# The end of a four-image attention and expert kernel in another order

## Chip, core and metric

The kernel runs on one core of one Trainium2 chip. Times are microseconds (us) of device time for the whole program. Engines are called as in the profile: PE (TensorE matmuls; PEld are its weight loads), DVE (VectorE), ACT (ScalarE), POOL (GpSimd), and SP, whose queue only issues transfers. A q behind a name (SPq) is the engine's queue. L497 is line 497 of the kernel before.

## What is computed

```python
# layer 0, x: (4, 32, 128, 128); 128 channels of 4096 positions per image
q = space_to_depth(x)                       # (b, 4096, 128) as the products use it
energy = q @ q.T / (|q_i| |q_j|)            # 4096 x 4096 per image, symmetric
x = gamma * (softmax(energy) @ q) + q       # turned back to (4, 32, 128, 128)
# layer 1, on 32 x 128 = 4096 rows (tokens) of 128 per image
t = t + linear_attention(ln(t))             # heads 8, out = Q (K^T V)
p, i = top_k(softmax(ln(t) @ router_w + router_b), 2); p = p / sum(p)
t = t + sum_k p_k * (ln(t) @ expert_w[i_k] + expert_b[i_k])      # 8 experts
```

All data are 32-bit floats. The attention of layer 1 is linear, so a Gram matrix of the normalised rows (128x128) stands for all of K^T V.

## The kernel before

**Four images in turn.** `attend(b)` does layer 0 of image b. It goes through the lower triangle of 512x512 blocks: a matmul into `pe` (L609), an exponential on ACT with row sums (L612), and two uses of the result: as weights for the values `po` (L497), and, turned by DVE (L421) and sent through DRAM on SP's queue (`blocks`, L530 and L545), for the mirrored block `pg` (L433). A mirrored block is used when a clock of planned PE work (`clock[0]`) has gone 57 units (`LAG`) past the issue of its transfer; a unit is about 0.25 us.

**Layer 1 beside it.** `layer1(b)` returns generators. While image b + 1 is in `attend`, layer 1 of image b is stepped every `PACE` = 10 units. For the last image (b = 3, `alone` in the code) there is nothing to hide it under: `close_rows` starts when its inputs are there, and `last_parts` comes after everything else. PE, DVE, ACT and SP run in the order in which the program issues (`manual_schedule`); on POOL, what is marked `pinned` keeps its order.

**Image 2 and the gathers.** For images 0 to 2, tokens are sorted by expert: POOL writes rows to DRAM with 32 scatters for each half of the rows (`DMA_INDIRECT`, L1053), SP loads them as tiles (L1083), PE multiplies each tile with its expert's weights (L1117), SP stores the results (L1103), and POOL gathers two results for each token (L1165). For image 2 (`b == B - 2`), `gather_apart` gathers into `yb`, eight for a group of four rows of tokens (`k`); DVE adds them to `acc` (L1200) and SP stores (`put`, L1159). Its second half (h = 1) has groups 4 to 7, so 32 gathers, and comes last. Every scatter and gather waits for the newest exponential (`exps`).

**The end of image 3.** The 32 rows `k` (128 tokens each) are closed in four batches of eight, kc = 0 to 3, by `close_rows`:

- denominators `den`, `rd`, `wide` (L747 to L752, DVE); transposes of them into `pbd` (L774, PE); `divide` into `df` (L761, DVE); the addition to T (L783); statistics (L786);
- `close_stats`: six small DVE operations (L682 to L688), then on POOL a power (L164) and one or two more (L690, L692), which give `rsa`, `nba` (or `rsf`, `nbf`, `nbo` for the second norm);
- `normalise` (ACT, L696) or, for four of the eight rows of kc = 2 and 3, a DVE operation (L796); the Gram product (L728) and its addition (L724); transposes to `xnT` (L701, copied by ACT, L714). `keep_running` (L186) fills PE with transposes that nobody reads.

`last_parts` then does, in program order: `matrix` (L839 to L843); attention of row groups u = 0 and 1 with their statistics (L854, L1309, L1317); of u = 2 and 3, copied by ACT to `copies` (L1311); logits of rows 0 to 15 (`router_rows`, 8 operations) and gates (`route(0)`, about 15); and the loop over k = 0 to 31. A step of the loop scales the eight products of row k with its gates: the last n = `by_scalar(k)` on ACT (L1247) and the rest on DVE (L1233). PE is two rows ahead with `py` (L1290, four matmuls of 0.43 us per row). Every second step POOL sums what ACT made (`sum_rows`, L1255 to L1259); every fourth, SP stores (L1265). Rows 16 to 31 get statistics, logits and gates from `second_half`, stepped once per k. The order of two pieces is plain from these lines:

```python
                if k < 8:
                    normalise(range(8 + k, 9 + k), rsf, nbo)
                    if k % 4 == 3:
                        transpose_tokens(2 + k // 4)()
                if k >= 1:
                    next(rest, None)
```

Of the kernel before, what the change touches and what calls it, by code (L numbers as in the profile page):

```python
# [22 lines left out]
def kernel(  # L23
# [43 lines left out]
    nc = tc.nc  # L67
# [586 lines left out]
    def layer1(b, st):  # L654
# [76 lines left out]
        def close_rows(kc):  # L731
# [18 lines left out]
            for s in range(2):  # L750
                one = rd[:, ts(s, NJ)][:, :, None]
                nc.vector.tensor_scalar(wide[:, :, s], one.to_broadcast([P, NJ, 64]), gam, None, ALU.mult)  # L752
            df = work.tile([P, 8, HW2, 2], F32, tag="df", name=f"df_{b}_{kc}", bufs=1)
# [31 lines left out]
            for j in range(8):  # L785
                stats[j]()  # L786
                if j == 3:
                    yield
                    yield
            close_stats("a", 8 * kc, 8, bs)  # L790
            yield from idle(1 if late_rows else 3)
            k = 8 * kc
            normalise(range(k, k + 4), rsa, nba)
            if late_rows:
                for j in range(k + 4, k + 8):
                    nc.vector.tensor_scalar(  # L796
                        xn[:, j, :D], T[:, j, :], rsa[:, j, :], nba[:, j, :], ALU.mult, ALU.add
                    )
            yield
            if last_rows:  # L800
                keep_running(36)
                done = gram_rows([k + j // 2 + 4 * (j % 2) for j in range(8)])
                yield
                done()
                return
# [70 lines left out]
        def route(h, temps=None):  # L876

            sh = [P, KT // 2, E]
            rows = slice(h * KT // 2, (h + 1) * KT // 2)
            ms, dn = (stat.tile([P, KT // 2, 1], F32, tag=nm, name=f"{nm}_{b}_{h}") for nm in ("ms", "dn"))  # L880
            pr = stat.tile(sh, F32, tag="prob", name=f"prob_{b}_{h}", bufs=1)
# [40 lines left out]
        def transpose_tokens(g, alloc=psum_t):  # L922

            pt, done = hold(
                f"ptf_{b}_{g}",
                lambda p: nc.scalar.activation(xn[:, ts(g, 4), :D], p.rearrange("p (j t) -> p j t", t=P), AF.Copy),
                alloc,
            )
            for j in range(4):
                nc.tensor.transpose(pt[:, ts(j, P)], xn[:, 4 * g + j, :D], ident)  # L930
            return done

        def attention_rows(u):
# [32 lines left out]
            if u % 2:  # L966
                for _ in route(u // 2):
# [6 lines left out]
        def sorted_experts(h):  # L974
# [72 lines left out]
            for n in range(2 * HR):  # L1047
# [14 lines left out]
                wait_for(inst.ins, exps, "not more of these at a time than steps have")  # L1062
                scatters.append(inst.ins)
# [97 lines left out]
            groups = list(range(r0 // 4, (r0 + HR) // 4))  # L1161

            def gather(to, g, i, j, op):
                k = 4 * g + j
                inst = nc.gpsimd.indirect_dma_start(to, None, ys, offset(place[:, i, k : k + 1]), compute_op=op)  # L1165
                wait_for(pinned(inst).ins, exps, "not more of these at a time than steps have")

# [17 lines left out]

            def gather_apart():
# [15 lines left out]

                for g in groups:
                    yb[g] = work.tile([P, 2, 4, D], F32, tag="wide", name=f"yb_{b}_{g}")
                    after_steps.append((now[0] + 1, partial(fetch, g)))
                    for n in range(8):
                        gather(yb[g][:, n // 4, n % 4, :], g, n // 4, n % 4, ALU.bypass)
                        if n == 7:
                            after_steps.append((now[0] + 4, partial(combine, g)))
                        if n % 2:  # L1210
                            yield
                            yield
                            due()
                turns[h].append("gathered")
# [23 lines left out]
        def scaled_rows(k, py, n=4):  # L1238

            if k % 2 == 0:  # L1240
                nm = f"tmp_{b}_{k // 2}"
                if n <= 4:
                    tmps[k // 2] = work.tile([P, 2, n, D], F32, tag="wide", name=nm)
                else:
                    tmps[k // 2] = fpool.tile([P, 2, n, D], F32, tag="F", name=nm)
# [15 lines left out]
        def store(g):  # L1261
            for r1 in range(2):
                for s in range(2):
                    p0 = s * 64 + r1 * 32
                    nc.sync.dma_start(dst[s, r1, :, ts(g, 4), :], accs[g][p0 : p0 + 32])  # L1265
# [9 lines left out]
        def last_parts():  # L1275
# [9 lines left out]
            def by_scalar(k):  # L1285

                return 6 if k < 8 else 5 if k < 14 else 4
# [4 lines left out]

            for _ in matrix():
                pass

            la = fpool.tile([P, KT, 2 * E], F32, tag="F", name=f"la_{b}")
            copies = {}

            def attended(u):
                if u >= 2:  # L1300
                    copies[u] = fpool.tile([P, 8, D], F32, tag="F", name=f"pac_{b}_{u}")
                for j0 in range(0, 8, 3):
                    pa = bank(f"pat_{b}_{u}_{j0}")
                    attend_rows(u, j0, pa)
                    nj = min(3, 8 - j0)
                    pr = pa[:, : nj * (D + 2 * E)].rearrange("p (j d) -> p j d", d=D + 2 * E)
                    if u < 2:
                        tg = T[:, 8 * u + j0 : 8 * u + j0 + nj, :]
                        nc.vector.tensor_tensor(tg, tg, pr[:, :, :D], ALU.add)  # L1309
                    else:  # L1310
                        nc.scalar.activation(copies[u][:, j0 : j0 + nj], pr[:, :, :D], AF.Copy)  # L1311
                    nc.scalar.activation(la[:, 8 * u + j0 : 8 * u + j0 + nj, :], pr[:, :, D:], AF.Copy)

            def stats_of(u):
                bs, stats = batch_stats("f", 8 * u, 8)
                for f in stats:
                    f()  # L1317
                close_stats("f", 8 * u, 8, bs)

            attended(0)  # L1320
            stats_of(0)
            transpose_rows(6)()
            transpose_rows(7)()
            attended(1)
            stats_of(1)
# [172 lines left out]
```

## Time and profile before

| what | value |
|---|---|
| median of 3 runs | 1663.79 us (1658.05 to 1667.66) |
| the profiled execution's own time | 1659.2 us |
| its span, first to last instruction | 1657.4 us |
| PE busy | 1623.1 us (98%), 5288 matmuls |
| DVE, ACT, POOL busy | 917.4, 910.4, 596.2 us |
| scatters and gathers on POOL | 192 of about 0.97 us; 128 of 1.59; 64 of 0.97 |

The page gives shares of the whole span. PE's share is high because layer 0 of the next image covers layer 1 of the one before; the last image has no such cover. What the end costs is therefore read from stretches of the span, each with its own limit: busy time of an engine close to the stretch's length marks the limit, and the waits say what the others wait for. PEclk is the share of PE's clock that was granted. PE's busy time includes filler transposes and is partly modelled.

### The profile page before, as it was taken

Reading aid. Unit: us, or ns where it says so; the run is one execution under the profiler, and the core shown is the slowest. Engines: PE = TensorE matmul, PEld = TensorE weight load, DVE = VectorE, ACT = ScalarE, POOL = GpSimd, SP = SyncE. Lnnn points to the kernel's source line nnn. Section 1 sums busy time; section 2 is a strip of 40 time slices with the busy share of each in tenths; the row PEclk is TensorE's granted clock in tenths of the full one; section 3 lists DMA queues with packets and bytes.
Section 4 is the critical chain, followed back from the end, with each engine's and each line's share of the span. In section 5 each row is a group of like instructions: output and inputs, shape, how many; then the busy total and the mean of one; then the engine's idle time right before and its main releaser. Section 6 shows DMA issues by size and latency. Waiting matters only on the chain.

```text
span 1657.4 us, 21471 instructions
## 1 busy us (share of the span) xinstructions
PE 1623.1 (98%) x5288; PEld 856.9 (52%) x5288; DVE 917.4 (55%) x2359; ACT 910.4 (55%) x2863; POOL 596.2 (36%) x565
## 2 busy tenths in 40 slices
PE   8999999999999999999999999999999999999987
PEld 5444544455554455555564455555565445554643
DVE  4543353567486443559378453448559533344686
ACT  3555445566575555556575455556657455555376
POOL 1000000001014531456555543346546642436166
PEclk9999999999999999999999999999999999999999
DMA  4555656665349776986778868797668877885001
GB/s 147 199 181 174 198 186 213 230 212 170 131 171 277 246 220 213 271 249 176 207 200 254 265 208 255 214 287 200 167 196 239 277 222 246 240 254 168 15 14 39
DMA packets 241899, 332.81 MB, mean 201 GB/s; under 512 B 31984, under 2 KB 168304, under 8 KB 227440
## 3 DMA queue, kind: packets, MB, share of 16 engines
q1 hardware_dynamic: 207312, 291.92, 55.5%
q0 software_dynamic: 26624, 25.58, 7.5%
q10 hardware_dynamic: 7840, 13.93, 2.8%
q8 instruction: 45, 0.74, 0.2%
q14 instruction: 78, 0.64, 0.1%
HBM read 160.78 MB, written 175.80 MB: 203 GB/s over the span
## 4 chain that ended last, share of the span: by engine, by line
PE 84%; DMA 4%; DVE 4%; SPq 3%; ACT 2%; issue 2%; another core or an unknown queue 1%; POOL 0%; ACTq 0%; DVEq 0%; POOLq 0%
PE po L497 24%; PE pe L609 23%; PE pg L433 20%; PE pys L1117 3%; DMA blocks<-F 3%; PE py L1290 3%; PE pg L453 2%; SPq L545 2%; PE pat L854 2%; PE pys L1124 2%; PE pgram L728 1%; PE ptx L701 1%; DVE df L761 1%; PE pgv L839 0%
## 5 line engine op out<-in xcount | busy, mean ns | idle before, releaser
L612 ACT ACTIVATE pr<-pe 128x512 f32<-128x512 f32 (+1 forms) x576 | 322.4, 560 | 544.0 <-PE pe L609 448.2
L497 PE MATMUL po<-pr,qT 128*128 128x512 f32 (+3 forms) x1152 | 549.6, 559 | 4.2 <-ACT o L502 3.0
L609 PE MATMUL pe<-qn,qn 128*128 128x512 f32 x896 | 459.6, 595 | 2.6 <-ACT pr L612 1.6
L433 PE MATMUL pg<-F,qT 128*128 128x512 f32 x880 | 449.7, 592 | 1.1 <-DMA F<-blocks 1.1
L421 DVE STREAM_TRANSPOSE F<-pr 128x512 f32<-128x512 f32 x440 | 305.9, 702 | 144.8 <-ACT pr L612 127.0
L497 PEld LDWEIGHTS po<-pr,qT 128*128 128x128 f32 x1152 | 215.3, 190 | 251.7 <-issue 221.2
L1165 POOL DMA_INDIRECT acc<-ys,place x128 | 203.2, 1588 | 215.8 <-ACT pr L612 140.3
L438 ACT ACTIVATE junk<-F 128x512 bf16<-128x512 f32 x440 | 273.0, 620 | 1.2 <-DMA F<-blocks 1.2
L433 PEld LDWEIGHTS pg<-F,qT 128*128 128x128 f32 x880 | 166.7, 190 | 195.4 <-issue 181.0
L1053 POOL DMA_INDIRECT xs<-xn,place x192 | 186.0, 969 | 189.7 <-ACT pr L612 116.6
L609 PEld LDWEIGHTS pe<-qn,qn 128*128 128x128 f32 x896 | 155.0, 191 | 115.0 <-issue 104.6
L442 DVE TENSOR_TENSOR o<-o,pg 128x512 f32<-128x512 f32 x110 | 75.3, 684 | 207.9 <-PE pg L433 173.4
L1099 DVE TENSOR_TENSOR results<-pys,xn 128x256 f32<-128x256 f32 x120 | 49.9, 416 | 187.1 <-ACT xn L1093 122.0
L164 POOL TENSOR_TENSOR rn<-ss,neg_half 128x8 f32<-128x8 f32 (+1 forms) x17 | 27.2, 1602 | 320.9 <-DVE ss L296 320.8
L612 ACT ACTIVATION_READ_ACCUMULATOR pr<-pe 128x1 f32 x576 | 112.0, 194 | 0.0
L1093 ACT ACTIVATE xn<-pys 128x256 f32<-128x256 f32 x120 | 45.2, 377 | 112.5 <-PE pys L1124 94.5
L1117 PEld LDWEIGHTS pys<-ew_sb,xn 128*128 128x128 f32 x468 | 70.4, 191 | 53.0 <-issue 49.5
L1165 POOL DMA_INDIRECT yb<-ys,place x64 | 61.8, 965 | 84.5 <-DMA F<-blocks 31.1
L609 PE MATMUL pe<-qn 128*128 128x512 f32 (+3 forms) x256 | 90.2, 435 | 0.7 <-ACT qn L342 0.7
L438 ACT ACTIVATION_READ_ACCUMULATOR junk<-F 128x1 f32 x440 | 84.6, 192 | 0.0
L1117 PE MATMUL pys<-ew_sb,xn 128*128 x468 | 71.7, 275 | 0.4 <-ACT xn L1093 0.4
L164 POOL TENSOR_TENSOR rsa<-dm_a,neg_half 128x8 f32<-128x8 f32 x16 | 28.9, 1807 | 103.1 <-DVE sv_a L688 102.9
(216 smaller groups left out, 1521.1 us busy)
## 6 DMA issues: line engine op xcount, KB each, us to landing
blocks<-F SPq DMA_DIRECT2D x110, 1024.0 KB
F<-blocks SPq DMA_DIRECT2D x220, 192.0 KB
F<-blocks SPq DMA_DIRECT2D x220, 128.0 KB
xn<-xs SPq DMA_DIRECT2D x114, 132.0 KB
ys<-results SPq DMA_DIRECT2D x114, 128.0 KB
F<-blocks SPq DMA_DIRECT2D x220, 64.0 KB
below<-F SPq DMA_DIRECT2D x31, 384.0 KB
T<-in_x_dram SPq DMA_DIRECT2D x64, 128.0 KB
```

Source lines behind the costliest of these rows:

```text
L164: pinned(nc.gpsimd.tensor_tensor(dst, src, neg_half.to_broadcast(list(src.shape)), ALU.pow))
L421: f()
L433: nc.tensor.matmul(pg.rearrange("p (a f) -> p a f", a=4), st["qT"][i][:, ib, :], G[:, :, ib], start=(ib == 0), stop=(ib == NJ - 1),)
L438: nc.scalar.activation(junk, G[:, :, ib], AF.Copy, accum_out=st["sums"][:, NJ * i + ib, jc : jc + 1])
L442: nc.vector.tensor_tensor(st["o"][jc], st["o"][jc], pg, ALU.add)
L497: nc.tensor.matmul(row["po"][:, lo:hi], qT[blk // NJ][:, blk % NJ, :], w, start=start, stop=(row["left"] == 0))
L609: nc.tensor.matmul(pe[:, c0:], qn[jc][:, ts(j, P)], qn[i][:, c0:], start=True, stop=True)
L612: nc.scalar.activation(pr[:, c0:], pe[:, c0:], AF.Exp, accum_out=sums[:, t, i : i + 1]).ins
L1053: inst = nc.gpsimd.indirect_dma_start(xs[h], offset(place[:, i, k : k + 1]), xn[:, k, :], None)
L1099: nc.vector.tensor_tensor(result[:, :n], p[:, 2 * P : 2 * P + n * D].rearrange("p (j c) -> p j c", c=D), bufs[g % 6][:, :n, D : D + 1].to_ ...
L1117: nc.tensor.matmul(p[:, 2 * P + j * D : 2 * P + j * D + D], bufs[6 + g % 2][:, j, :D], weights[:, bass.ds(begins[2 * (g % 2) + j], D)], st ...
L1165: inst = nc.gpsimd.indirect_dma_start(to, None, ys, offset(place[:, i, k : k + 1]), compute_op=op)
```

## The change

For image 3: batch kc = 2 holds its statistics back until kc = 3 has its denominators; ACT normalises all eight rows of kc = 2 and three of kc = 3 (DVE the other five); the filler falls from 36 to 10 transposes; Gram products take eight rows at a time. For image 2: group 7's eight gathers and half of group 6's leave `gather_apart` and are issued in `close_rows` of image 3, four in kc = 2 and eight in kc = 3; their additions and stores go into the last loop; every fourth scatter or gather waits for the four before it. In `last_parts`, gates come for rows 0 to 7 first, for 8 to 15 in steps 4 to 7 of the loop, and for 16 to 31 in steps 10 to 15. GpSimd normalises rows 2 to 15 and adds the `copies`; ACT takes six experts for k below 16 and four from there; the last stores go over two queues.

```diff
 def close_rows(kc):
...
+            if last_rows:
+                st["all_divided"] = True
...
+            while late_rows and "all_divided" not in st:
+                yield from idle(1)
             close_stats("a", 8 * kc, 8, bs)
-            yield from idle(1 if late_rows else 3)
+            if late_rows:
+                for _ in range(8 if last_rows else 4):
+                    states[b - 1]["gathers"].pop(0)()
+            yield from idle(1 if alone else 3)
             k = 8 * kc
-            normalise(range(k, k + 4), rsa, nba)
-            if late_rows:
-                for j in range(k + 4, k + 8):
+            normalise(range(k, k + (3 if last_rows else 8 if late_rows else 4)), rsa, nba)
+            if last_rows:
+                for j in range(k + 3, k + 8):
                     nc.vector.tensor_scalar(
...
             if last_rows:
-                keep_running(36)
-                done = gram_rows([k + j // 2 + 4 * (j % 2) for j in range(8)])
+                keep_running(10)
+                done = gram_rows([k + j for j in (3, 0, 4, 1, 5, 2, 6, 7)])
                 yield
                 done()
+                return
+            if late_rows:
+                done = gram_rows(range(k, k + 8))
+                turned = [transpose_rows(g) for g in (4, 5)]
+                yield
+                for done in (done, *turned):
+                    done()
                 return
...
-        def route(h, temps=None):
+        def route(r0, nr, temps=None):
...
-        def transpose_tokens(g, alloc=psum_t):
+        def transpose_tokens(k0, n):
...
+                if b == B - 2 and n % 4 == 0:      # scatters
+                    wait_for(inst.ins, scatters[-4:], "a pause after each fourth")
...
+                if b == B - 2 and j == 0:          # gathers
+                    wait_for(inst.ins, gathered[-4:], "a pause after each fourth")
+                gathered.append(inst.ins)
...
+            def fetch_late(g):
+                accs[g] = buffer("acc", g)         # in the pool of pr
+                nc.sync.dma_start(accs[g], t2[:, ts(g, 4)])
...
+            def leave_for_the_end(g):
+                made = []
+                gathers.extend(partial(gather_late, g, n, made) for n in range(8))
+                gathers[-8:] = [lambda f=gathers[-8]: (fetch_late(g), f())] + gathers[-7:]
+                sums_left.extend(partial(add_late, g, lambda i=i: made[i]) for i in range(2))
+                sums_left.append(partial(put, g))
...
+                if h == 1:
+                    leave_for_the_end(groups.pop())
...
+                        if apart and n == 4:       # the last group that is left
+                            break
...
+                if h == 1:
+                    leave_half_for_the_end(groups[-1], yb[groups[-1]])
...
-                return 6 if k < 8 else 5 if k < 14 else 4
+                return 6 if k < 16 else 4
...
+            transpose_rows(6)()
             for _ in matrix():
                 pass
+            transpose_rows(7)()
...
+            bs0, stats0 = batch_stats("f", 0, 8)
+            bs1, stats1 = batch_stats("f", 8, 8)
+            for j0 in (0, 3, 6):
+                attended(0, j0)
+            some_stats(stats0, 0)
+            some_stats(stats0, 4)
+            close_stats("f", 0, 8, bs0)
+            logits = router_rows(nc.vector, 0, 8, la[:, :8])
+            next(logits)
+            for u in (1, 2):
+                for j0 in (0, 3, 6):
+                    attended(u, j0)
+            normalise(range(0, 2), rsf, nbo)
+            pinned_rows = range(2, 8)
+            normalise_apart(pinned_rows)           # nc.gpsimd.tensor_scalar, a row each
+            for _ in logits:
+                pass
+            attended(3, 0)
+            attended(3, 3)
+            transpose_tokens(0, 2)()
+            attended(3, 6)
+            gates = route(0, 8)
+            next(gates)
+            for u in (2, 3):
+                tg = T[:, ts(u, 8), :]
+                pinned(nc.gpsimd.tensor_tensor(tg, tg, copies[u], ALU.add))
+            products = [product(0, h, bank(f"py_{b}_0_{h}")) for h in range(2)]
+            transpose_tokens(2, 2)()
+            some_stats(stats1, 0)
+            for _ in gates:
+                pass
+            transpose_tokens(4, 4)()
+            products += [product(1, h, bank(f"py_{b}_1_{h}")) for h in range(2)]
...
+            rest = rest_of_rows()                  # stats1, close, stats, router, route(8, 8), ...
+            left = list(states[b - 1]["gathers"]) + list(states[b - 1]["sums_left"])
             for k in range(KT + 4):
+                if 2 <= k < 6:
+                    normalise_apart(range(4 + 2 * k, 6 + 2 * k))
...
+                    if k in (4, 6):
+                        transpose_tokens(2 * k, 4)()
...
-                    store(k // 4 - 1)
+                    store(k // 4 - 1, (nc.sync, nc.scalar) if k > KT else (nc.sync, nc.sync))
...
+                if 11 <= k < 25:
+                    normalise(range(2 * k - 6, 2 * k - 4) if k < 13 else range(k + 7, k + 8), rsf, nbo)
+                if k in (12, 16, 20, 24):
+                    transpose_tokens(k + 4, 4)()
+                if 17 <= k and left:
+                    left.pop(0)()
+                next(rest, None)
```

## Prediction

> **What bounds the kernel now.** I read the page's first part, then a table of stretches over the last 155 us, then the waits, the chain of waits and the timeline inside each stretch. The page has TensorE (PE) busy for 1623.1 of 1657.4 us, and the timeline shows fewer than 12 us of PE gaps (over 0.25 us each) before 1500 us. So nothing done before 1500 us can give much, and the question is what the end is worth:
>
> ```profile
> core 0: us, PE busy (x) PEld busy (x) DVE busy (x) ACT busy (x) POOL busy (x), PEclk, DMA share, GB/s
> 1502.00:1547.50 45.50, 42.08 (x131) 21.65 (x131) 29.79 (x80) 24.90 (x78) 24.79 (x25) 0.96 0.38 106
> 1547.50:1565.90 18.40, 15.29 (x105) 13.65 (x103) 11.67 (x38) 7.47 (x17) 2.78 (x4) 0.91 0.06 15
> 1565.90:1570.40 4.50, 3.96 (x23) 3.10 (x23) 1.59 (x4) 0.51 (x1) 0.00 (x0) 1.00 0.01 4
> 1570.40:1588.50 18.10, 15.91 (x96) 12.12 (x96) 15.77 (x64) 9.45 (x31) 4.76 (x6) 1.00 0.00 0
> 1588.50:1602.80 14.30, 12.56 (x29) 4.33 (x30) 13.19 (x39) 13.16 (x48) 9.60 (x9) 1.00 0.04 10
> 1602.80:1621.60 18.80, 17.37 (x45) 6.40 (x44) 14.34 (x48) 17.02 (x57) 17.75 (x21) 1.00 0.13 30
> 1621.60:1650.80 29.20, 27.88 (x70) 12.15 (x68) 22.42 (x64) 22.63 (x79) 23.51 (x27) 1.00 0.18 41
> 1650.80:1657.40 6.60, 0.00 (x0) 0.00 (x0) 1.54 (x3) 0.00 (x0) 0.00 (x0) 0.67 0.18 41
> ```
>
> I put the borders at events: the last value matmul (1547.5), the last Gram sum (1565.9), the first attention matmul (1570.4), and rows 0, 8 and 16 of the expert loop. In 1570–1588 DVE leads (15.8 of 18.1). In the loop's first half ACT leads (13.2 of 14.3, 17.0 of 18.8) with POOL beside it; in its second half PE leads. A busy PE is partly filler: the chain has
>
> ```profile
> 1558.79 5.00 PE spare L186 x36
> 1563.79 1.80 PE pgram L728 x16
> ```
>
> where the rows for the Gram product were ready at 1562.4 (end of the four ACT rows of L696).
>
> In the first stretch, the waits of 1515–1530 are
>
> ```profile
> DVE df L761 <- remote: 5.4, 1, 5.4
> ACT pr L612 <- PE pe L609: 4.7, 1, 4.7
> ...
> ACT pr L612 <- remote: 3.3, 1, 3.3
> ```
>
> DVE and ACT were freed within 0.05 us of each other at 1528.05, though the matmuls they waited for stand at 1523.3–1523.7: the news of the matmuls came late. Each ACT wait of over 2.6 us between 1285 and 1530 has seven or more gathers or scatters in the 12 us before it, mostly 1.25–1.3 us apart. The gathers of 1416–1468, mostly alternating 1.25 and 2.0 us, have no such wait. PE lost 1.0 us (at 1502) and 2.4 us (at 1527) by it, and then
>
> ```profile
> 1526.70:1530.10 3.40, 1.04 (x6) 0.58 (x5) 2.02 (x3) 2.00 (x10) 1.06 (x2) 1.00 0.07 20
> 1530.10:1533.50 3.40, 3.34 (x8) 1.59 (x7) 3.32 (x6) 2.34 (x8) 2.79 (x3) 0.50 0.21 58
> ```
>
> a window 31% busy is followed by one at clock 0.50, another 1.7 us.
>
> **What the Trainium skill says.** "TensorE: Matmul & The Clock Gate", Part 1, has the PE clock halved after an idle window of about 3.4 us; the lines above agree in length and halving, except that here 31% busy counted as idle. "SBUF — State Buffer", "SBUF: two separate sides", calls the port pair of DVE and GpSimd an exclusive lock: a DVE operation with two SBUF inputs and a GpSimd operation shut each other out for a whole instruction. The trace agrees:
>
> ```profile
> 1596.95 1.80 POOL L1255 TENSOR_TENSOR tmp<-tmp 128x768 f32<-128x768 f32 x1
> 1596.96 1.84 DVE L684 TENSOR_TENSOR dm_f<-bs_f 128x16 f32<-128x16 f32 x1
> ...
> 1599.05 0.59 DVE L686 TENSOR_TENSOR dm_f<-dm_f,sv_f 128x16 f32<-128x16 f32 x1
> ```
>
> L684 takes 0.17 us for 8 rows with POOL idle; these six operations took 3.8 us instead of 0.95, or 0.7 us for each of the four with two inputs.
>
> **The change, step by step** (gain positive, us).
>
> (1) Gathers. Twelve of the last 32 gathers (12 x 1.25 = 15 us of POOL) leave the time before 1533, and each fourth scatter and gather of image 2 waits for the four before it. Price of a pause: a gather ended its issue at 1525.99 and the last semaphore update after it stands at 1527.26, so 1.3 us less the usual 0.3. Behind it on POOL stand the powers L164 of close_rows; behind the scatters SP's loads xn<-xs (L1083) and then F<-blocks. Scatters of half 0 may end 7 us later, which SP's transfers bear if the 57 clock units before their use (about 14 us) hold. If late news goes: 1.0 + 2.4 + 1.7 = 5.1, with the 1.9 us of gaps at 1324–1349, 7.0. If a pause makes F late: −2. Nothing in the trace shows four gathers and a stop; I take 4.5, as the mean spacing comes to 1.5.
>
> (2) Denominators first. The division of rows 24–31 stood at 1551.5, since DVE waited with four rows (L796) for POOL's nba, and ACT copied o (L502) after its own four. Now o comes at 1547.6, and the division follows the transposes of rdx at about 1549.0: 2.5. The filler falls from 36 to 10, and ACT has three rows and DVE five (1.4 us): the Gram sum ends 0.3 us after the last row instead of 3.2: 3.0. Rows 16–23 all go to ACT, whose idle (11 of 18.4 us) covers the four more. Against it, these windows stay lean and a half clock may hit Gram and matrix: 0 to 1.7. I take 4.5 (3 to 6).
>
> (3) Eight gathers on POOL after nba: 8 x 1.25 + 1.0 = 11 us, from about 1558 to 1569 on the new time axis; the power for rows 0–7 is due at 1570. 0 to 3 late; −0.5.
>
> (4) First gates. From the first attention matmul to the loop was 18.1. Off the path go the statistics of rows 8–15 (1.57 + 0.95) and a part of each gate operation (128 elements 0.29, 64 I estimate at 0.22: some 20 operations, 1.4). But the exponential now stands behind ACT's copies for u = 2 and 3, two rows and a copy of two: ready at 12.0 instead of 13.5, the 13 operations after it 3.0 instead of 4.1, so 15.1. GpSimd's addition to T (128x1024, 2.3 by the slope of L1255, 1.27 at 512 and 1.81 at 768) may lock one out: −1 to 3; I take 1.5.
>
> (5) Rows 0–7 of the loop, 14.3 before. ACT loses its rows (8 x 0.45) and would need 8 x 1.63 + 1.2 = 14.2. But DVE has 8 x 0.74 sums, 16 statistics (3.4), a close (0.95), and the logits and gates of rows 8–15, 8 + 15 operations of 0.22 to 0.25: 15.6. Of these 18 have two SBUF inputs, while POOL sums n = 6 pairs (1.81 + 3 x 0.73 = 4.0). The full lock price is 18 x 0.7 = 12.6; none would be 0. I take a third, 4.2, as pair 0 isn't there before 4 us and normalising rows on GpSimd are short: "GPSIMD Engine Reference", "Engine selection", has one-input operations at roughly line rate; no such row of 128x128 is in the trace, and I estimate 0.3 from the 0.19 left at zero length on the L1255 slope plus 128 elements at 1.2 GHz (0.45 at two-input speed). 19.8, so −5.5 (−13 to 0).
>
> (6) Rows 8–15, 18.8 before: 16.6 of ACT (48 scaled rows and seven normalised), with close and gates on DVE at 17.3: 1.5. Rows 16–31, 29.2: PE needs 14 x 1.72 + 1.3 + 1.1 = 26.5; I take 27.2, so 2. POOL's 59 us in the whole loop end in time because rows from 16 on cost it 1.36 each; if not, the three acc buffers stop DVE.
>
> (7) Last stores over two queues: four issues of 0.65 in turn become two: 1.3.
>
> At nothing: transposes 6 and 7 (8 x 0.11, under the Gram copy and the gv copies); four additions (0.69) and eight stores of image 2 from row 17 on, under DVE's third of free time there and an idle SP; two fetches of acc from ACT's queue (0.33 each) to SP's, which has nothing due. Without that cover the additions cost 2.8.
>
> Sum: 4.5 + 4.5 − 0.5 + 1.5 − 5.5 + 3.5 + 1.3 = 9.3. The profiled execution took 1659.2 (span 1657.4 and 1.8 around it), 4.6 below the median; off the median of 1663.8 that is 1654.5.
>
> **Rivals.** *Free lock*: DVE slips between POOL's instructions, step 5 costs 1.3 and the clock holds. For it: L685 ran at 0.17 between two POOL sums. 9.3 + 4.2 + 1 = 14.5: 1649. *Pauses don't cure the news*: the lateness comes from the amount of gathers, not from their run, or from something else late at the end of attention; step 1 gives 0 and half the lock price is paid: 9.3 − 4.5 − 2.1 = 2.7: 1661. *Slower*: the gates of rows 8–15 come late. At row 4, PE's transposes of rows 8–11 wait for POOL, which is in pair 0 (until about 10) and has rows 10 and 11 behind it; ACT waits for its copy, POOL is never empty, and each of the 18 operations pays 0.7. Then row 8 starts at 15.6 + 12.6 + 5 = 33 instead of 19.8: 9.3 − 13.4, and the power for rows 16–31, queued behind two pair sums (2 x 4.0), holds ACT at row 11 by 5 more: −9.1, 1673. The balance tips when row 8 starts more than 29 us after row 0. *Not what it says*: gathers in a lump of eight on POOL still hold back PE's news, now in the Gram stretch; that is inside steps 2 and 3.
>
> **Numbers.** 0.5% (8.3 us) is about what a measurement of this kernel tells from no change. Forecast 0.45 (by itself 1649 to 1658; four fifths of it beyond 0.5%), free lock 0.18, pauses without cure 0.23, slower 0.14 (0.10 of it beyond, and 0.02 of the case before it). Faster 0.54, same 0.34, slower 0.12. The range 1643 to 1668 leaves out some of the free lock's and of the slower case's far ends.
>
> **What would show it.** No ACT wait above 3 us for PE before the last exponential (1); the df operations of rows 24–31 within 2 us of the last value matmul, no chain in spare (2); rsf of rows 0–7 right behind sv_f (3); loop start 16 to 17 us after the first pat (4); row 8 at 18 to 22 us from row 0, with DVE operations of 0.6 us and more beside L1255 (5). Wrong it is if row 8 comes after 29 us or the late news stays.

## The result, and the profile after

The changed kernel took 1679.1 us, the median of six runs (1677.95 to 1683.16). The kernel before took 1663.9, also the median of six (1658.05 to 1667.66). The ratio is 1.0101, 95% interval 1.0077 to 1.0125: slower by 1%, where 1654.5 had been forecast and the range ended at 1668. On another chip, where the kernel before took 1651.0, the ratio was 1.0141 (1.0124 to 1.0158), so the loss there is 23 us. The profiled execution of the changed kernel took 1683.2 (span 1681.4), the longest of its six, and that of the kernel before lay under its median. So the two traces differ by 24.0 us of span where the medians differ by 15.2; the 24.0 us divide like this (longer is positive; the forecast column has the prediction's steps at their places, steps 2 and 3 in the second row):

| stretch | before | after | change | forecast |
|---|---|---|---|---|
| start to the last value matmul | 1547.7 | 1565.2 | +17.5 | −4.5 |
| last value matmul to last Gram sum | 18.2 | 13.1 | −5.1 | −4.0 |
| last Gram sum to the first attention matmul | 4.5 | 4.4 | −0.1 | 0 |
| first attention matmul to row 0 | 18.1 | 17.7 | −0.4 | −1.5 |
| row 0 to row 8 | 14.3 | 25.3 | +11.0 | +5.5 |
| row 8 to row 16 | 18.8 | 19.0 | +0.2 | −1.5 |
| row 16 to row 31 | 27.2 | 27.3 | +0.1 | −2.0 |
| row 31 to the end | 8.6 | 9.4 | +0.8 | −1.3 |

The table of stretches of the changed kernel, with borders at the same events (the last Gram sum at 1578.3, the first attention matmul at 1582.7, rows 0, 8 and 16 at 1600.4, 1625.7 and 1644.7). PEclk is the share of PE's clock that was granted:

```profile
core 0: us, PE busy (x) PEld busy (x) DVE busy (x) ACT busy (x) POOL busy (x), PEclk, DMA share, GB/s
1502.00:1565.10 63.10, 45.77 (x151) 24.61 (x150) 27.52 (x78) 25.07 (x78) 18.62 (x20) 0.84 0.23 68
1565.10:1578.30 13.20, 9.09 (x67) 7.70 (x65) 8.89 (x31) 7.22 (x16) 10.02 (x10) 1.00 0.10 25
1582.70:1600.40 17.70, 14.28 (x83) 10.63 (x82) 13.55 (x49) 6.63 (x25) 13.26 (x15) 1.00 0.06 15
1600.40:1625.70 25.30, 18.13 (x40) 6.98 (x40) 23.29 (x63) 14.37 (x51) 20.57 (x27) 0.87 0.05 11
1625.70:1644.70 19.00, 16.96 (x34) 6.67 (x34) 13.66 (x51) 15.88 (x57) 15.62 (x16) 0.81 0.13 29
```

Two rows stand out. In the first, PE is busy for 45.8 of 63.1 us at a clock of 0.84, where it had been busy for 42.1 of 45.5 at 0.96. In the fourth, DVE is busy for 23.3 of 25.3 us; it had 13.2 of 14.3.

**The first loss, 17.5 us.** The waits of the changed kernel from 1505 to 1530 (engine and line, what it waited for, us in total, times, longest):

```profile
ACT xn L696 <- POOL nba L690: 19.7, 1, 19.7
PE pgram L728 <- ACT xn L696: 17.3, 1, 17.3
POOL yb L1183 <- DMA yb<-ys,place: 7.9, 3, 3.3
```

One wait of ACT accounts for the whole loss: the normalise of batch kc = 0 waited for POOL's `nba`, and since ACT runs in order, the exponentials behind it stopped, and PE with them. The timeline of the changed kernel shows what POOL did (bracket: idle time before, and what ended it; L688 on DVE makes the input of the power L164):

```profile
1509.66 0.94 POOL L1183 DMA_INDIRECT yb<-ys,place  x1 [3.29 <-DMA yb<-ys,place]
...
1514.13 0.23 DVE L688 TENSOR_SCALAR sv_a<-sv_a 128x8 f32<-128x8 f32 x1
...
1516.63 0.94 POOL L1183 DMA_INDIRECT yb<-ys,place  x1 [2.29 <-DMA yb<-ys,place]
...
1523.61 0.94 POOL L1183 DMA_INDIRECT yb<-ys,place  x1 [2.29 <-DMA yb<-ys,place]
...
1525.82 1.68 POOL L164 TENSOR_TENSOR rsa<-dm_a,neg_half 128x8 f32<-128x8 f32 x1
1527.58 0.20 POOL L690 TENSOR_TENSOR nba<-sv_a,rsa 128x8 f32<-128x8 f32 x1
1527.82 1.65 ACT L696 ACTIVATE xn<-T,nba,rsa 128x128 f32<-128x128 f32 x4 [19.74 <-POOL nba L690]
```

In the kernel before, the same place reads

```profile
1510.22 0.94 POOL L1165 DMA_INDIRECT yb<-ys,place  x1 [0.31 <-issue]
...
1511.06 0.17 DVE L688 TENSOR_SCALAR sv_a<-sv_a 128x8 f32<-128x8 f32 x1
...
1511.24 1.67 POOL L164 TENSOR_TENSOR rsa<-dm_a,neg_half 128x8 f32<-128x8 f32 x1
```

Between pauses the gathers stand 1.25 apart. The power stands behind 18 gathers of the second half in both kernels. Before, it followed its input at once, at 1511.2. Here its input was ready at 1514.4, and it stood 11.5 us longer behind gathers, until 1525.8.

**The second loss, 11 us.** Rows 4 to 8 took 18.4 us instead of 8.8. In the timeline of the changed kernel inside them, POOL's pair sums (L1310) and two-input DVE operations of 64 elements start together and end together:

```profile
1608.36 1.81 POOL L1310 TENSOR_TENSOR tmp<-tmp 128x768 f32<-128x768 f32 x1
1608.49 1.76 DVE L882 TENSOR_TENSOR lw<-lw,sda 128x64 f32<-128x64 f32 x1
...
1622.24 1.80 POOL L1310 TENSOR_TENSOR tmp<-tmp 128x768 f32<-128x768 f32 x1 [1.01 <-ACT tmp L1302]
1622.32 1.80 DVE L925 TENSOR_TENSOR second<-second,weight 128x64 f32<-128x64 f32 x1
```

The same operations take 0.22 us when POOL is idle. Added up over the logits and gates of rows 8 to 15, what they took above 0.22 is 9.6 us, as much as the difference of rows 4 to 8.

### The profile page after: what moved, and what is told of

Its sections match the earlier page's. It is cut to its first block, busy times and chain, and to the rows that moved or that the text cites. A ratio compares the mean times of both kernels' runs of the same rounds, so it can differ in the third digit from the quotient of the medians.

```text
span 1681.4 us, 21419 instructions
## 1 busy us (share of the span) xinstructions
PE 1620.8 (96%) x5256; PEld 853.4 (51%) x5256; DVE 923.8 (55%) x2367; ACT 910.0 (54%) x2864; POOL 609.0 (36%) x582
## 5 line engine op out<-in xcount | busy, mean ns | idle before, releaser
L164 POOL TENSOR_TENSOR rn<-ss,neg_half 128x8 f32<-128x8 f32 (+1 forms) x17 | 27.3, 1603 | 319.8 <-DVE ss L296 319.7
L1183 POOL DMA_INDIRECT yb<-ys,place x56 | 54.3, 970 | 95.0 <-DMA F<-blocks 31.1
L1345 PE MATMUL py<-ew_sb,xn 128*128 128x512 f32 x128 | 65.3, 651 | 12.0 <-DVE bs_f L1372 5.4
```

The costliest lines, as they stand in the source:

```text
L1345: nc.tensor.matmul(bank, xn[:, k, :D], ew_sb[:, 4 * h : 4 * h + 4, :], start=True, stop=True)
```

## The experiments

The theory after these readings: pauses cost by what stands behind them on POOL, and the loop pays most of the price of the lock between DVE and POOL. The rivals: the moved gathers or the other order of the batches put the power late; and DVE simply has too much to do in rows 0 to 8. The kernel before differs by chip: 1649.9 us beside e1 to e4; 1651.0 beside before_again, after_again, e5, e6; 1661.0 beside e7 to e10; 1650.7 beside e12 and the repeats. So ratios are taken to the kernel before on the same chip, and traces are compared among chips near 1650.

### e1: no pause between gathers

```diff
-                if b == B - 2 and j == 0:
-                    wait_for(inst.ins, gathered[-4:], "a pause after each fourth")
```

> The changed kernel without the pause between image 2's gathers (scatters keep theirs, twelve gathers stay moved). Theory (the pauses hold POOL, so that the power of batch kc = 0, which stands behind 18 gathers, starts at 1525.8 instead of 1511.2, and ACT, PE and the last exponential go with it): the power back at 1511 to 1513, the last exponential at 1545 to 1549 instead of 1563.2, the rest of the end as in the changed kernel, 1661 to 1666 us. Rival (the gathers or the other order of the end, not their pauses, put the power late): the power stays after 1520 and the time at 1675 to 1680. Second rival (the pauses also cured late news, worth 3.4 us): the last exponential returns to 1549 at best and the time to 1665 to 1668.

Measured: 1657.8 us, ratio 1.0055 (1.0038 to 1.0073). The power is back at 1503, the last exponential comes at 1538.4, and at 1555.9 in the changed kernel on a chip with the same time before: 17.5 us, as the theory had it (its forecasts in us were made from the chip with 1664). The rest of the loss stays: from the last exponential to the end 117.0 us.

### e2: the pause alone

```diff
+                if b == B - 2 and j == 0:
+                    wait_for(inst.ins, gathered[-4:], "a pause after each fourth")
```

> The kernel before, with only the pause between image 2's gathers added (all 32 gathers of the second half stay where they are, scatters without pauses). Theory (a pause costs 2 to 3 us of POOL and what stands behind it is the power): the last exponential at 1560 to 1570 instead of 1545.8, 1676 to 1688 us; the end behind it keeps the length that it had before. Rival (the pause costs nothing by itself; the loss lies in the moved gathers or the denominators held back): 1658 to 1664, with no ACT wait above 3 us for PE.

Measured: 1666.0 us, ratio 1.0098 (1.0080 to 1.0116). The last exponential comes at 1550.4, 15.2 us later than in the kernel before (before_again), and from there to the end it takes 112.9 us, as before (112.5). The waits of e2 from 1497 to 1537 show the same chain as in the changed kernel:

```profile
ACT xn L696 <- POOL nba L690: 12.7, 1, 12.7
POOL yb L1166 <- DMA yb<-ys,place: 12.4, 5, 4.8
PE pgram L728 <- ACT xn L696: 10.3, 1, 10.3
```

The absolute forecast (1676 to 1688) was made from the chip with 1664; against 1650 the 16 us are those expected.

### e3 and e4: gates of rows 8 to 15 in PSUM

```diff
+                temps = psum_t("gates8").rearrange("p (n k e) -> p n k e", n=4, e=E)[:, :, :8]
-                logits = router_rows(nc.vector, 8, 8, la[:, 8:16])
+                logits = router_rows(nc.vector, 8, 8, la[:, 8:16], temps)
...
-                gates = route(8, 8)
+                gates = route(8, 8, temps)
```

e4 has this and e1's edit.

> The changed kernel with the gates of rows 8 to 15 kept in PSUM while they are worked out, as those of rows 16 to 31 are; nothing else is changed. Theory (two-input DVE operations are shut out by POOL's pair sums; 9.6 us above their free time in rows 4 to 8): these operations back at 0.22 us each, row 8 at 16 to 18 us after row 0 instead of 25.3, the time 7 to 9 us lower, 1670 to 1672. Rival (DVE has too much to do in these rows whoever else runs, or POOL's sums are what ACT waits for): row 8 stays above 22 us after row 0 and the time within 3 us of 1679.

> Both edits: no pause between gathers, and the gates of rows 8 to 15 in PSUM. If the two losses are separate they add: 1663 less 8 is 1653 to 1657, below the kernel before. If the first edit brings late news back in the end or the second only moves the wait to POOL's sums behind row 8: 1660 to 1666.

Measured: e3 1672.6 us, ratio 1.0136 (1.0119 to 1.0153); e4 1656.1, 1.0036 (1.0022 to 1.0051). Row 8 comes 16.4 (e3) and 17.0 us (e4) after row 0 instead of 25.3: the lock was the cause of these 9 us, and DVE does not have too much to do. But from the last exponential to the end only 3.3 us were gained (after_again, below, to e3) and 4.1 (e1 to e4), and in the ratios 0.8 and 3.1, where 7 to 9 had been forecast. e4 is above the kernel before and not below it, as it should have been if the two losses add. The timeline of e4 has the same line beside the same pair sum:

```profile
1585.43 1.81 POOL L1308 TENSOR_TENSOR tmp<-tmp 128x768 f32<-128x768 f32 x1
1585.53 0.23 DVE L882 TENSOR_TENSOR gates<-gates,sda 128x64 f32<-128x64 f32 x1
...
1586.71 0.62 DVE L885 TENSOR_TENSOR gates<-nbf,srw 128x64 f32<-128x64 f32 x1
```

L882 now has one input in PSUM and runs at 0.23 us beside POOL; L885 still has both inputs in SBUF and is held until 1587.3, just after the pair sum ends. That is what the Trainium skill, "SBUF — State Buffer", "Who interferes with whom", says of the second input: it comes through the read interface shared with GpSimd.

Rows 8 to 16 show where most of the 9 us went. They took 23.4 (e3) and 22.8 us (e4) instead of 17.9 (after_again). In e4:

```profile
1600.04 0.16 DVE L688 TENSOR_SCALAR sv_f<-sv_f 128x16 f32<-128x16 f32 x1
1602.39 2.93 POOL L164 TENSOR_TENSOR rsf<-dm_f,neg_half 128x16 f32<-128x16 f32 x1
1605.71 0.36 POOL L692 TENSOR_SCALAR nbo<-nbf 128x16 f32<-128x16 f32 x1
1606.10 0.88 ACT L696 ACTIVATE xn<-T,nbo,rsf 128x128 f32<-128x128 f32 x2 [1.67 <-POOL nbo L692]
```

The power for rows 16 to 31 is ready to run at 1600.2, waits until POOL has ended a pair, and takes 2.9 us; meanwhile the pair sums wait. POOL is busy for 21.9 of the 22.8 us there, so POOL is taken for the new bound; e10 below tests that in part.

### before_again and after_again: the two kernels on one chip

> The kernel before once more, for a trace from the same chip as the experiments. The chips differ: the kernel before took 1663.8 us in the first runs and 1649.9 beside the first experiments. Theory: the 14 us lie in the stretch after 1485 us of image 3, where news of matmuls comes late beside gathers, and the last exponential comes at about 1532 here; the length from the last exponential to the end is the same 111.6 us to within 1. Rival: the 14 us are spread over the whole program, and the stretch from 1485 to the last exponential is 60 us long as in the first trace.

> The changed kernel once more, beside the others. From the third experiment (1672.6 with row 8 at 16.4 us from row 0 instead of 25.3, of which 4.4 were given back by row 16) it should take 1676 to 1679 on the chip where the kernel before takes 1650, 27 us more; the first ratio, 1.0101, would give 1667. The end from the last exponential takes 118 us.

Measured: before_again 1649.6 us (one run) with the last exponential at 1535.3, 112.5 us ahead of the end. after_again 1674.3, a little under its forecast, ratio 1.0141 (1.0124 to 1.0158), 116.3 us from the last exponential to the end. It has the same two losses: 20.6 us at the last exponential, 9.9 in rows 0 to 8.

The trace of before_again also takes away the prediction's reading of the late news. Its waits of ACT from 1280 to 1530, over the same scatters and gathers, are

```profile
ACT pr L612 <- PE pe L609: 62.5, 55, 1.9
ACT xn L1093 <- PE pys L1124: 34.3, 34, 1.2
```

None is longer than 1.9 us, where the first trace had seven of 3.2 to 5.8, though 14 gathers stand 1.25 us apart here from 1506 to 1523. Of the 10.5 us between the two traces of the same kernel, 1.8 arise in the first 190 us, 3.1 beside the scatters from 1285 to 1353, and 5.6 after 1485, so the expectation, which had all of it after 1485, was half right. A run of seven or more gathers does not make news late by itself; it did so in the first runs and beside e7 to e10 only, and why is open.

### e5 and e6: the order of the batches, and the old loop

e5 is the kernel before with the edits of `close_rows` alone, that is the new order of kc = 2 and 3 and one line more (`idle`); e6 is e1 with `last_parts` as before. The diff is that of e5, cut.

```diff
+            while late_rows and "all_divided" not in st:
+                yield from idle(1)
...
-            yield from idle(1 if late_rows else 3)
+            yield from idle(1 if alone else 3)
-            normalise(range(k, k + 4), rsa, nba)
+            normalise(range(k, k + (3 if last_rows else 8 if late_rows else 4)), rsa, nba)
...
-                keep_running(36)
+                keep_running(10)
```

> The kernel before with only the new order of the batches kc = 2 and 3: denominators first, all eight rows of kc = 2 and three of kc = 3 on ACT, 10 filler transposes instead of 36, Gram products of eight rows. No pause, no moved gather, the loop as before. Theory: the stretch from the last value matmul to the last Gram sum, 18.2 us before and 13.1 in the changed kernel, is 13 to 14 here, the rest is unchanged, and the time falls by 4 to 6 us, ratio 0.9965 to 0.9975. Rival (what is gained there is lost to PE's clock in Gram and matrix, or to batch kc = 2 held back): ratio above 0.999.

> The changed kernel without the pause between gathers and with last_parts as before (gates of 16 rows ahead of the loop, rows normalised by ACT, old split of experts), with the twelve moved gathers, their additions and the last stores over two queues kept. Theory (the loss is the pauses and the new loop): from the last exponential to the end 105 to 107 us against 111.6 before and 118.2 after, the time 4 to 8 us under the kernel before if the moved gathers also spare POOL before the last exponential, ratio 0.995 to 0.998. Rival (moving the gathers is itself the loss, since the first experiment without pauses was still 8 us above the kernel before): the last exponential comes 4 to 7 us later than in the kernel before on the same chip, and the ratio is 1.000 to 1.003.

Measured: e5 1649.4 us, ratio 0.9992 (0.9984 to 1.0001); e6 1649.25, 0.9993 (0.9984 to 1.0001). In e6 the last exponential is 106.6 us ahead of the end, as expected, against 117.0 in e1: the new `last_parts`, with its loop, costs 10.4 us. In e5 the stretch from the last value matmul to the last Gram sum took 12.5 us instead of 18.0, a gain of 5.5. And yet neither is faster, since the last exponential came 5.2 (e5) and 3.2 us (e6) later. One line tells why, in the timeline of e6; the kernel before has no such wait:

```profile
1505.25 1.65 ACT L696 ACTIVATE xn<-T,nba,rsa 128x128 f32<-128x128 f32 x4 [3.44 <-POOL nba L690]
```

The diff has an edit that the prediction passed over: `idle(1 if late_rows else 3)` became `idle(1 if alone else 3)`, so that in kc = 0 and 1 as well, ACT reaches its normalise one step after the statistics and not three. The power itself runs at the same time (1503.3 in e6, 1503.6 in before_again), and ACT stands waiting for it. e8_again below has this edit alone: its last exponential comes 5.4 us later, as in e5, and its stretch to the last Gram sum is 2.9 us shorter than before.

### e7 to e10: the three steps back, the one step alone, a lighter split

e7 is e6, e9 the changed kernel, each with this edit; e8 is the kernel before with the reverse; e10 is e4 with this edit and, second diff, a lighter split of experts.

```diff
-            yield from idle(1 if alone else 3)
+            yield from idle(1 if late_rows else 3)
```

```diff
-                return 6 if k < 16 else 4
+                return 6 if k < 4 else 5 if k < 16 else 4
```

> The kernel of e6 (no pause, old last_parts, twelve gathers moved, denominators first) with the wait of three steps instead of one between close_stats and normalise in batches kc = 0 and 1, as in the kernel before. Theory (with one step ACT reaches the normalise of kc = 0 before POOL has the power; it waited 3.4 us for nba in e5 and 3.5 in e6, 0 in the kernel before): no ACT wait for nba there, the last exponential 3 to 3.5 us earlier, ratio 0.9965 to 0.9980, below both kernels. Rival (PE has enough queued to bridge those 3.4 us, and the later exponential of e5 and e6 comes from kc = 2 held back): ratio above 0.9985.

> The kernel before with only the wait between close_stats and normalise in batches kc = 0 and 1 cut from three steps to one. Theory: ACT waits 3.4 us for nba of kc = 0, PE runs dry for about 1 us and slips by 3 to 3.5 us against the blocks, the last exponential 3 to 4 us later, ratio 1.0015 to 1.0025. Rival (no harm by itself): within 1.000 plus or minus 0.0008.

> The changed kernel, pauses and all, with three steps instead of one between close_stats and normalise in kc = 0 and 1. Theory (the harm is the pause and the early normalise together: ACT waited 18.1 us for nba in the changed kernel, 12.7 in the kernel with the pauses alone): the wait falls to about 12.7, the last exponential comes 5 us earlier, 1668 to 1670 us where the changed kernel takes 1674. Rival (the power is late by the pauses alone, and what ACT does in those two steps is done later anyway): within 2 us of 1674.

> The changed kernel without the pause between gathers, with three steps in kc = 0 and 1, gates of rows 8 to 15 in PSUM, and ACT taking five experts instead of six in rows 4 to 15, so that POOL sums 3.5 us per pair instead of 4.0. Theory (in e4 rows 8 to 16 took 22.8 us, because POOL's backlog of pair sums put the power for rows 16 to 31 late): rows 8 to 16 in 19 to 20.5 us, row 0 to row 8 still 16 to 18, and the time 5 to 8 us under e4, that is 0.998 to 1.001 of the kernel before. Rival (DVE is the bound there, which takes one expert more): rows 8 to 16 stay at 22 us or more.

Measured, on a chip with late news: e7 1654.5 us, ratio 0.9963 (0.9948 to 0.9979), faster than both kernels. Its ACT still waited 2.4 us for `nba` of kc = 0, which the expectation excluded.

e8 1661.1, 1.0001 (0.9989 to 1.0013), though ACT waited 5.8 us for `nba`: on this chip the ACT of e8 also waited 5.9 us at 1503 for late news, and the cost did not show.

e9 1671.3, 1.0064 (1.0042 to 1.0086), with 15.9 us of wait instead of 18.1 and the last exponential at 1551.7 instead of 1555.9 in after_again. That agrees in size, but the changed kernel was not run on this chip, so the difference in time is not settled.

e10 1661.0, 0.9999 (0.9987 to 1.0011), 0.0037 below e4, but on a chip with late news and with the three steps back, so how much of this is the split is not settled. Row 8 came 17.1 us after row 0 as expected, but rows 8 to 16 took 21.5, between both forecasts. POOL was busy for 20.0 of them, and the small operations of `close_stats` were locked again (L684 took 1.3 us), so that the power started at 1609.6. What else bounds these rows is not settled.

### e12 and the repeats

e12 is e2 with one more condition, set where `close_stats` of image 3's first batch is issued.

```diff
             close_stats("a", 8 * kc, 8, bs)
+            if alone:
+                st["closed"] = True
...
-                if b == B - 2 and j == 0:
+                if b == B - 2 and j == 0 and "closed" in states[b + 1]:
```

> The kernel before with the pause between image 2's gathers only from where close_stats of kc = 0 of image 3 has been issued, so that most of the pauses of e2 (all that stand ahead of that power on POOL) are gone and some three pauses behind it stay. Theory (a pause costs by what stands behind it; three pauses of 2.4 us end before the power of kc = 1 is due, for which POOL waited 5.3 us in the kernel before): ratio 0.999 to 1.001, no ACT wait for nba above 3 us. Rival (every pause costs its 2 to 3 us wherever it stands): ratio 1.003 to 1.005; e2 had 1.0098.

Measured: 1650.1 us, ratio 0.9995 (0.9986 to 1.0003). In its timeline the power comes at 1506.9, and the pauses stand behind it, at full length:

```profile
1506.91 1.68 POOL L164 TENSOR_TENSOR rsa<-dm_a,neg_half 128x8 f32<-128x8 f32 x1
...
1521.22 0.94 POOL L1168 DMA_INDIRECT yb<-ys,place  x1 [2.30 <-DMA yb<-ys,place]
...
1528.60 0.94 POOL L1168 DMA_INDIRECT yb<-ys,place  x1 [2.38 <-ACT pr_back L590]
```

Three pauses of 2.3 to 2.5 us cost nothing that can be measured where nothing urgent stands behind them; at 2 us each they would have cost 0.004. The one wait for `nba` above 3 us, 3.83 at 1552.6, is the one that the kernel before has too (3.84 at 1550.4).

e8_again, e7_again and e11 on the same chip; e11 is e5 with three steps kept, and no gather moved.

> e8 once more: only one step instead of three between close_stats and normalise in kc = 0 and 1. On a chip where the kernel before lies near 1650 us: ratio 1.0015 to 1.0025 if the early normalise costs its 3.4 us of ACT wait, 1.000 plus or minus 0.0008 if PE bridges it. On a chip where the kernel before lies near 1661 to 1664, where PE stands still there for late news anyway, both theories give 1.000.

> e7 once more (denominators first, twelve gathers moved without pauses, old loop, three steps). If its gain is the Gram stretch's 5 us: ratio 0.996 to 0.9975 on any chip. If it came from late news that moved gathers spare: 0.998 to 1.000 on a chip near 1650 us.

> The kernel before with only the new order of kc = 2 and 3 (denominators first, ACT for all rows of kc = 2 and three of kc = 3, 10 fillers) and three steps kept in kc = 0 and 1; no gather is moved. If moving gathers is worth nothing: the same as e7_again to within 0.0008. If the moved gathers free POOL (and SP) before the last exponential, or the twelve disturb the Gram stretch: e7_again lies 1 to 3 us lower, or higher.

Measured: e8_again 1652.4, ratio 1.0010 (1.0001 to 1.0019), with a wait of 3.6 us for `nba`: the early normalise costs something by itself, about 1.7 us (0.2 to 3.1), less than forecast. Where the three steps came back, e5 to e11 gained 0.0027 and e6 to e7_again 0.0014 (4.5 and 2.3 us, between chips near 1650).

e7_again 1647.5, 0.9979 (0.9970 to 0.9988), between its two forecasts. e11 1645.9, 0.9965 (0.9953 to 0.9977). The two profiled spans are the same, 1644.4 us, but the median of e7_again is 1.6 us higher, outside the 0.0008 that was to mean no difference. So moving the twelve gathers gains nothing here; whether it costs 1 to 2 us is not settled, as the intervals overlap. e11, a small part of the change, is the best version found, 4.8 us under the kernel before, and its stretch to the last Gram sum takes 13.8 us instead of 18.0: the order of the batches gains 4.2 by itself.

The ratios divide the loss of 23 us near 1650: taking out the pauses (after_again to e1) gives back 14.2 us, the old `last_parts` (e1 to e6) 10.2, the three steps (e6 to e7_again) 2.3, gathers and stores as they were (e7_again to e11) 2.3, which is the part not settled; and the order of the batches, which stays in e11, gains 5.8.

## Why the prediction was wrong, step by step

Gains are positive here, as in the prediction.

**Step 1, forecast +4.5, was −17.5.** Three things failed. First, the price of a pause: 1.0, from the 1.3 us between the end of a gather's issue and its last semaphore update in the trace. In the changed kernel, the last gather ahead of the pause at 1523.6 is issued from 1520.37 to 1521.32, its last update comes at 1522.84, and the next gather starts at 1523.61. So 1.5 us go until it has landed and 0.8 more until the next one starts, which the price left out. POOL waits 2.3 us instead of 0.3, and a pause costs 2.0 at least; the pauses between 1420 and 1510 took 2.5 to 7.4, with other waits among them. The Trainium skill, "DMA: Bandwidth & Descriptors", "Anatomy of one DMA — SWDGE (gpsimd) path", gives about 2.0 us of fixed cost for a transfer from GpSimd; the trace has 2.5 from the start of this gather's issue to its last update, and that page was not used for this price.

Second and larger, who stands behind. The prediction wrote "Behind it on POOL stand the powers L164 of close_rows" and then priced only SP's loads. The pauses ahead of the power add up in it. Half 0's gathers ended 15.6 us later, but POOL had stood idle for 16.3 us between the halves in the kernel before, so half 1 began only 4.5 us later (1489.7 instead of 1485.2). The four pauses in half 1 made the other 10.1: from its first gather to the power it took 36.1 us instead of 26.0. Together the power came 14.6 us late. e2 shows that the pauses alone cost 15.2 us at the last exponential, e12 that behind the power they cost nothing.

Third, the edit from three steps to one in kc = 0 and 1 was not costed at all. e5, e6 and e8_again put it at 1.7 to 4.5 us. With the pauses, ACT waits 18.1 us for `nba` in after_again; in e2 and e9, which kept three steps, 12.7 and 15.9.

And the gain came in part at most. On chips near 1650 no news is late. On the first chip the stalls beside the scatters (1300 to 1337, 3.6 to 5.1 us each) stayed in the changed kernel, but there no pause came about: its scatters still stand 1.27 us apart in runs of eight and more. The edit puts the wait into the code, but the trace shows no pause; why is open. Beside the gathers no ACT wait for PE above 2.6 us is left in the two traces with pauses from chips with late news (the changed kernel and e9), where the kernel before, e7, e8 and e10 have such waits of up to 5.9. So the pauses may have cured that part; ACT's own stop for `nba` falls into the same stretch, and no run separates the two.

**Steps 2 and 3, forecast +4.0 together, were +5.1.** Right; the order alone, in e11, gives 4.2, and about 1 comes with the single step. The division of the last batch starts 0.9 us after the last value matmul (3.8 before), and e5, e7 and e11 keep 3.9 to 5.5 us with the old loop. The eight gathers of step 3 ended at 1587.8, and the power for `rsf` of rows 0 to 7 started at 1588.0, right behind its input from DVE: no cost.

**Step 4, forecast +1.5, was +0.4.** GpSimd's two additions to T took 4.65 us together, the 2.3 each that had been estimated, but they locked out two gate operations (L908 1.24 and L910 2.02 us instead of 0.22): 2.8 us. The step had named −1 to 3 for its gain, by this lock, and took 1.5.

**Step 5, forecast −5.5, was −11.0.** The mechanism was right: DVE's work, and a lock price on top. The share of the price was wrong: a third of 12.6 was taken, three quarters (9.6) were paid. That the forecast work of 15.6 and the 9.6 make 25.2, where 25.3 was measured, is partly luck: DVE was busy for 23.3 us, so its work without the lock was 13.7, and it stood idle for 2.0. The prediction's own table had DVE busy for 13.19 of 14.3 us in these rows, as long as ACT (13.16); it named ACT alone as leading, and then gave DVE more. DVE seldom slips between POOL's instructions, since POOL is busy for 20.6 of 25.3 us and each sum holds the ports for its whole length.

**Step 6, forecast +3.5, was −0.3; step 7, forecast +1.3, was −0.8.** In the first two traces nothing was gained from row 8 on, with PE's clock at 0.81 up to row 16, which the sum did not have. In after_again, at a clock of 1.00, rows 8 to 16 took 17.9 us instead of 18.8 in before_again and rows 16 to 31 26.6 instead of 27.2, so about 1.5 of the 3.5 can be had. From the last DVE operation to the end it took 4.9 us before, 5.7 after, 4.9 in e11 (one queue) and 5.0 in e7_again (two): the four issues in a row were not what the end waited for. The 0.8 goes with the new loop: row 31 to the end takes 9.4 in every trace with it and 8.6 or 8.7 in every trace with the old one. Why is open.

**The rivals.** The slower one came nearest in time (1673), and it had named POOL's lag, but at rows 8 to 15; row 8 came at 25.3, short of the 29 us from which it was to decide. The loss was at a place that no rival had: POOL ahead of the first batch. "Pauses don't cure the news" is not decided, as step 1 says, and it was wrong that the pauses then cost 0. "Free lock" is ruled out by the 9.6 us. The prediction's own sign, that the late news stays, came in part: beside the scatters.

## What to carry to other kernels

Before a wait is put on an in-order queue, list what stands behind it up to the next result that another engine needs, and charge that result with every pause ahead of it, less the idle time in between, not with one pause; e2 has 14 pauses, 11 of them ahead of the power, and 1.0098, while e12 has only the three behind it and 0.9995. A lock that two engines share is paid for the most part, here three quarters, when one of them is busy for 81% of the time. Giving one operand another home (here PSUM) took 9 us off these rows, but only 3 to 4 off the end, so look next at who becomes the bound. And a change of many parts is worth taking apart: its one good part, e11, is 0.9965.

## What the runs showed of the hardware

The kernel before took 1650 to 1651, 1661 or 1664 us in different sets of runs, on several chips. Between the two traces of it, 8.7 of the 10.5 us up to the last exponential lie where scatters and gathers run, in waits of ACT of 3 to 6 us that the trace from the 1650 us chip does not show at all. A 128x128 normalise on GpSimd with two per-partition factors took 0.45 us, where 0.3 had been estimated. In the changed kernel PE's clock was 0.67 in the 10 us from 1510 and 0.50 in the 10 us from 1520, while PE waited 17 us for the normalise, and 0.81 in the next 10 us. A DVE operation with both inputs in SBUF (L882) ended with the GpSimd pair sum beside it, after 1.76 us instead of 0.22; with one input in PSUM it took 0.23 us beside such a sum.
